# Two attention layers and experts on one core: slots of exp tiles chosen by the planner, and layer 1's softmax sums on TensorE

## The chip, the core and the metric

The kernel runs on one core of one Trainium2 chip. A core has five engines that work side by side and wait for each other by semaphores: TensorE (PE: matmuls, and PEld for loading weights), VectorE (DVE), ScalarE (ACT), GpSimd (POOL) and SyncE (SP, which here only issues DMAs). TensorE writes to PSUM; the other tiles lie in SBUF. The metric is the device time of one execution in microseconds (us).

## The reference

The input x is 8 images of 256 channels and 32 x 32 pixels, all in float32. Layer 0 is attention of 8 heads of 32 channels, with keys and values from x at four pooled sizes (1024 + 256 + 121 + 25 = 1426 places). Layer 1 is attention of one head of 256 channels over the 1024 pixels as tokens, followed by eight experts of three products each, weighted by a gate that is taken from the mean over the images. Cut to what matters:

```python
# layer 0, after a group norm of x; k and v: pooled, convolved, layer-normed
attn = softmax(einsum('bhqd,bhkd->bhqk', q_g, k) * 32 ** -0.5)
out_att = einsum('bhqk,bhkd->bhqd', attn, v)
...                                   # mixed by a small constant attention, then projected
x = x + out
# layer 1
t = tokens(x)
t = t + softmax(q1 @ k1.T * 256 ** -0.5) @ v1        # q1, k1, v1 from layernorm(t)
h = relu(bn(layernorm(t) @ W1[e])); h = relu(bn(h @ W2[e])); y = h @ Wo[e]
t = t + sum over e of gate[f, e] * y
```

## The kernel before

Almost every instruction is recorded through one object, Flow, so the profile gives nearly all of them the same line (L671, inside Flow's call); a reader goes by tile names and not by lines. Flow keeps a clock for each engine (`now`), and for each tile a time at which it will be ready and one at which it will have been read. Flow.cost prices an instruction; Flow.transfer prices a DMA. Every engine executes its instructions in the order in which they are recorded.

Layer 0's scores are the backbone. The loop at the end of `attention` runs over image b, head group c (four heads), half of the queries (512) and key chunk kc (up to 128 places). A step records `scores`: four products into the single PSUM tile sc, and one exp of 128 x 2048 into a tile pt. One step later it records `values`: four products into pv with the exps as operand. There are 352 such exps, and 8 of the last 18 keys (ptail). The softmax sum over the keys needs the exp tiles added up: the odd chunk's tile is added onto the even chunk's by a GpSimd DMA with accumulation (`add`), VectorE adds the pairs (`sums`), and a product with ones sums over the partitions. `normalise` turns that total into rec (transpose, reciprocal of 16 columns, transpose) and multiplies att by it. pt has six slots. An exp tile's slot comes free when its last reader is done: the adding DMA for an odd tile, a VectorE add for an even one, the ones-product for the first.

Between the steps, Flow.step lets other threads record work as filler: convolutions and keys for the next image (VectorE's taps on acc), queries, the projection, and all of layer 1 as far as its input is there. A thread yields what it needs next, an engine and tiles, and is resumed when Flow's clock says that these are near; TensorE's filler is limited by a credit for each step. Flow.finish records whatever is needed until a condition holds.

Which slot a new tile gets is decided in two places. Flow.tile assumes, for its own account, the slot that comes free first. The tile pool, which only knows that a tag has six slots, places the tile itself, and nothing ties the two together.

Layer 1 runs as two threads. `layer1` normalises tokens, makes v and y, and records for each of 32 blocks of 256 queries four exp tiles p1 of two key chunks each (tag p1, six slots). `outputs` sums them: four VectorE adds into s, one product with ones, a reciprocal of 128 x 256 from PSUM; then the products with v, the multiplication by the reciprocal, the residual, a store, and the norm. In both layers ScalarE sums up the totals and their reciprocals by Copy with accum_out into the tables hi and lo; at the end of the kernel these are compared with a limit, and a general path runs if a value is too large.

When the last scores are done, the experts begin, interleaved with what is left of layer 1. Until the gates are known, expert layers are computed ahead, each as four products of 512 columns, and kept in DRAM (h2d); afterwards most are seven products of 256 columns (Strassen's scheme) with sums on VectorE. The expert part works on the banks named bank and y.

Of the kernel before, what the change touches and what calls it, by code (L numbers as in the profile page):

```python
# [36 lines left out]
NEAR = {"DVE": 1.5, "ACT": 2.0, "POOL": 1.0, "SP": 10.0}  # L37
BUFS = {"sm": 2, "sx": 1}
# [15 lines left out]
class Kit:  # L54
# [6 lines left out]
    def tile(self, pool, shape, tag, bufs=None):  # L61
        self.n += 1
        return pool.tile(shape, F32, tag=tag, name=f"{tag}_{self.n}", bufs=bufs)
# [594 lines left out]
class Flow:  # L658
# [27 lines left out]
    def __init__(self, tc, kit):  # L686
# [10 lines left out]
        self.threads = []  # L697
        self.cut = {}
# [6 lines left out]
    def tile(self, pool, shape, tag, bufs=1):  # L705
        t = self.kit.tile(pool, shape, tag, bufs=bufs)
        slots = self.slots.setdefault(tag, [None] * bufs)
        i = min(range(bufs), key=lambda i: self.end(slots[i]))
        self.ready[t.name] = self.end(slots[i])
        slots[i] = t.name  # L710
        if tag in BUFS:
            self.open.add(t.name)
        return t

# [51 lines left out]
    def note(self, engine, op, ins, args, kwargs):  # L766
# [35 lines left out]
        if "dma" in op:  # L802
            both = out.space == DRAM and srcs[0].space == DRAM
            size = 4e-3 * out.shape[0] * out.free_size() if out.space != DRAM else 4e-3 * srcs[0].shape[0] * srcs[0].free_size()
            lag = self.transfer(engine, end, size * (0.0054 if engine == "POOL" or both else 0.003))
# [8 lines left out]
    def transfer(self, queue, at, work):  # L814
# [10 lines left out]
        return 1.7 + left[mine] + min(left[mine], left[other]) + self.served - at  # L825
# [88 lines left out]
def attention(tc, kit, f, outer, ended, nb, consts, x, t1, t2, hn, bounds, vecs, q_t, kv_t, proj_t, gqk_t, wqk, wqkv, vecs1, w1_d, w1c, gate_d, wrc, vecs2, bnvec, w2_d, h2d, between, pre, held):  # L914
# [6 lines left out]
    with ExitStack() as ctx:  # L921
# [41 lines left out]
        ident, grp = kit.ident, con[:, K_GRP : K_GRP + P]  # L963
        heads = T(l1, [P, P + DH], "res", bufs=2)
# [28 lines left out]
        def mix():  # L993
# [48 lines left out]
            yield ve(wa)  # L1042
            rs = T(wp, [P, 2], "wars")
# [24 lines left out]
            yield ve(ps)  # L1068
            raw = T(l1, [P, 2, C], "s")
# [111 lines left out]
        pmaps = [T(pool_, [P, NK], f"p{i}") for i, pool_ in enumerate((between, work))]  # L1181
# [70 lines left out]
        def first_keys(half):  # L1252
# [3 lines left out]
            for m in range(2):  # L1256
# [15 lines left out]
                f.act.activation(acc[:, half * 512 : half * 512 + 512], ps, AF.Identity, bias=db(m, 0))  # L1272
            large.append(("keys", half))
# [326 lines left out]
        def sums(n, pairs):  # L1600

            for i in range(1, NKC // 2):
                yield until(lambda: len(pairs) > i)
                for j in range(0, 4, 2):
                    s = pairs[0][:, j : j + 2, :]
                    yield ve(s, pairs[i])
                    f.ve.tensor_tensor(s, s, pairs[i][:, j : j + 2, :], ALU.add)
            yield until(lambda: normalised[0] == n)
            yield pe(pairs[0], tag="sm")
            total = small()  # L1610
            for j in range(4):
                f.pe.matmul(
                    total[DH * j : DH * j + DH, :], lhsT=kit.ones[:, :DH], rhs=pairs[0][:, j, :], start=True, stop=True
                )
            return total

        def normalise(b, c, sl, total, n):
# [5 lines left out]
            f.act.activation(total, total, AF.Copy, accum_out=hi[:, column[n] : column[n] + 1])  # L1623
            one = T(work, [P, 16, 1], "one")
            f.ve.reciprocal(one, turned[:, :, 0:1])
            f.ve.transpose(turned, one.to_broadcast([P, 16, DH]))
            f.ve.tensor_tensor(att, att, rec, ALU.mult)
            yield act(rec)
            f.act.activation(rec, rec, AF.Copy, accum_out=lo[:, column[n] : column[n] + 1])

        def project(b):
            if b == nb - 1:
                last = T(work, [P, 2, HW], "pt", bufs=6)
                f.sp.dma_start(last, x[b].rearrange("(k p) n -> p k n", p=P))
# [19 lines left out]
            if b == nb - 1:  # L1654
                f.sp.dma_start(t1[b], last)
            projected[0] += 1
# [92 lines left out]
        def outputs():  # L1749

            for i in range(4 * nb):
# [5 lines left out]
                s = T(l1, [P, 2, C], "s")  # L1757
                yield ve(*p1[:2])
                f.ve.tensor_tensor(s, p1[0], p1[1], ALU.add)
                for g in range(2, 4):  # L1760
                    yield ve(p1[g])
                    f.ve.tensor_tensor(s, s, p1[g], ALU.add)
                f.ve.tensor_tensor(s[:, 0, :], s[:, 0, :], s[:, 1, :], ALU.add)
                yield pe(s, tag="sm")
                ps = small()
                f.pe.matmul(ps[:, :C], lhsT=kit.ones, rhs=s[:, 0, :], start=True, stop=True)
                yield ve(ps)
                rec = T(l1, [P, C], "rec1")
                n = 8 * (i // 4) + 4 + i % 4
                f.act.activation(ps[:, C:], ps[:, :C], AF.Copy, accum_out=hi[:, n : n + 1])  # L1770
                f.ve.reciprocal(rec, ps[:, :C])
# [980 lines left out]
```

## Time and profile before

| | us |
|---|---|
| median of 3 runs (3258.67 to 3266.59) | 3259.01 |
| the profiled execution | 3261.05 |
| its span, first to last instruction | 3259.2 |
| TensorE busy with matmuls | 3056.5 |
| VectorE busy | 2406.7 |
| ScalarE busy | 1682.6 |
| GpSimd busy | 1240.7 |

Layer 0's scores run from 78 to about 1900 us of the span, the experts' banks from 2013 on. In the trace every float32 product appears as two records (two passes), so counts of matmuls there are twice those of the program. A product with 32 weight columns is marked 128*32; four of them run side by side in the array's column groups. In lists of waits, a line names who waited, for whom, the total, how often, and the longest. In tables by stretches, each engine's busy time is followed by its number of records; PEclk is the mean granted share of TensorE's clock.

### The profile page before, as it was taken

How to read it: one execution, taken by the hardware profiler on the slowest of the kernel's cores; microseconds unless marked ns; L12 is line 12 of the kernel's file. 1: busy time of each engine (PE TensorE's matmuls, PEld its weight loads, DVE VectorE, ACT ScalarE, POOL GpSimd, SP SyncE). 2: the span in 40 equal slices, each digit the busy share in tenths (PEclk: the TensorE clock that was granted, in tenths of full speed). 3: DMA queues.
4: the chain of work that ended last, by engine and by line, in shares of the span. 5: the costliest groups of instructions: out<-in, count | busy, mean ns of one | idle time of the engine just before them, and what ended most of it. 6: DMA issues, size and time to landing. Idle time of an engine off the chain costs nothing.

```text
span 3259.2 us, 55911 instructions
## 1 busy us (share of the span) xinstructions
PE 3056.5 (94%) x22330; PEld 1789.3 (55%) x22330; DVE 2406.7 (74%) x4117; ACT 1682.6 (52%) x2301; POOL 1240.7 (38%) x1327
## 2 busy tenths in 40 slices
PE   8778799999979989989999999999999999999998
PEld 4322234334325334424333356777888888888887
DVE  5886786987877888969754544447888887777776
ACT  4566566666645657657665533333333334444443
POOL 3211413224222232232121112007655667777776
PEclk9899999999989999989999999999999999999999
DMA  1376657665664565565676645225444430000000
GB/s 54 86 153 156 125 124 155 137 148 111 141 145 84 128 151 113 137 143 111 141 182 126 144 111 207 94 88 171 146 149 149 149 117 20 20 20 33 20 14 21
DMA packets 115710, 368.68 MB, mean 113 GB/s; under 512 B 14305, under 2 KB 40233, under 8 KB 92209
## 3 DMA queue, kind: packets, MB, share of 16 engines
q0 software_dynamic: 28608, 179.85, 28.5%
q1 hardware_dynamic: 83472, 183.19, 16.7%
q8 instruction: 178, 2.92, 0.4%
q10 hardware_dynamic: 3360, 1.97, 0.2%
q14 instruction: 92, 0.75, 0.1%
HBM read 116.12 MB, written 83.40 MB: 61 GB/s over the span
## 4 chain that ended last, share of the span: by engine, by line
PE 49%; DVE 6%; DMA 3%; issue 2%; ACT 2%; POOL 1%; SPq 0%; DVEq 0%; POOLq 0%; ACTq 0%
PE bank L671 20%; PE y L671 10%; PE sm L671 9%; PE sx L671 4%; PE sc L671 3%; PE pv L671 3%; DVE h L671 2%; DMA pt<-pt 2%; ACT pt L671 1%; DVE acc L671 1%; DVE u L671 1%; DVE c L671 1%; DVE pt L671 1%; DVE t L671 0%; DMA t<-res 0%
## 5 line engine op out<-in xcount | busy, mean ns | idle before, releaser
L671 ACT ACTIVATE pt<-sc 128x2048 f32<-128x2048 f32 x352 | 660.9, 1877 | 296.7 <-PE sc L671 204.3
L671 DVE SCALAR_TENSOR_TENSOR acc<-p,vec,acc 128x961 f32<-128x961 f32 (+3 forms) x960 | 562.2, 594 | 35.1 <-ACT acc L671 9.4
L671 PE MATMUL sc<-q,kn 32*128 32x512 f32 (+1 forms) x3072 | 428.5, 662 | 125.1 <-ACT pt L671 121.8
L671 DVE TENSOR_TENSOR pt<-pt,pt 128x1024 f32<-128x1024 f32 x320 | 391.9, 1271 | 148.3 <-DMA pt<-pt 123.7
L671 PE MATMUL pv<-pt,vt 128*32 128x512 f32 x2816 | 390.9, 628 | 1.7 <-ACT vt L671 1.2
L671 ACT ACTIVATE h<-h,bnvec 128x512 f32<-128x512 f32 x450 | 340.4, 805 | 61.8 <-DVE h L671 53.1
L671 ACT ACTIVATE p1c<-bank 128x256 f32<-128x256 f32 x225 | 86.2, 383 | 553.5 <-PE bank L671 553.2
L671 POOL TENSOR_TENSOR rstd<-rstd,mhalf 128x4 f32<-128x4 f32 (+2 forms) x88 | 106.6, 1211 | 651.6 <-DVE rstd L671 560.2
L671 POOL DMA_DIRECT2D pt<-pt x160 | 146.3, 916 | 465.4 <-ACT pt L671 376.7
L671 DVE TENSOR_TENSOR h<-p1c,bank 128x512 f32<-128x512 f32 x225 | 153.3, 682 | 200.2 <-PE bank L671 196.5
L671 PEld LDWEIGHTS sc<-q,kn 32*128 32x128 f32 (+1 forms) x3072 | 115.7, 182 | 324.4 <-ACT pt L671 223.2
L671 POOL TENSOR_TENSOR tm<-h,tm 128x256 f32<-128x256 f32 x208 | 239.2, 1150 | 16.3
L671 DVE TENSOR_TENSOR h<-u,bank 128x256 f32<-128x256 f32 x450 | 229.2, 550 | 7.7
L671 PEld LDWEIGHTS pv<-pt,vt 128*32 128x32 f32 x2816 | 56.3, 109 | 281.3 <-issue 262.1
L671 POOL TENSOR_TENSOR tm<-h 128x512 f32<-128x512 f32 x104 | 133.2, 1281 | 202.6 <-ACT h L671 198.5
L671 DVE TENSOR_TENSOR h<-h,gate 128x1024 f32<-128x1024 f32 x128 | 199.9, 1561 | 0.5 <-ACT h L671 0.5
L671 PE MATMUL y<-t,s3e 128*128 128x256 f32 x768 | 187.0, 379 | 3.1 <-POOL t L671 1.7
L671 PE MATMUL bank<-t,s1e 128*128 128x256 f32 x726 | 178.1, 381 | 2.6 <-DVE t L671 2.4
L671 POOL TENSOR_TENSOR t<-h,t 128x256 f32<-128x256 f32 x214 | 169.5, 792 | 16.8
L671 POOL TENSOR_TENSOR t<-h 128x512 f32<-128x512 f32 x107 | 136.1, 1272 | 98.1 <-DVE h L671 77.4
L671 DVE TENSOR_TENSOR u<-h,bank 128x512 f32<-128x512 f32 x225 | 154.7, 688 | 24.7 <-PE bank L671 1.4
L671 PEld LDWEIGHTS y<-t,s3e 128*128 128x128 f32 x768 | 145.7, 190 | 24.0 <-POOL t L671 2.5
(376 smaller groups left out, 5557.5 us busy)
## 6 DMA issues: line engine op xcount, KB each, us to landing
pt<-pt POOLq DMA_DIRECT2D x160, 1024.0 KB, 7.7
h<-h SPq DMA_DIRECT2D x123, 512.0 KB
xi<-in_x_dram SPq DMA_DIRECT2D x16, 512.0 KB
t<-t SPq DMA_DIRECT2D x8, 1024.0 KB
res<-t SPq DMA_DIRECT2D x32, 256.0 KB
t<-res SPq DMA_DIRECT2D x32, 256.0 KB
hn<-res SPq DMA_DIRECT2D x32, 256.0 KB
hn<-hn SPq DMA_DIRECT2D x16, 512.0 KB
```

Source lines behind the costliest of these rows:

```text
L671: ins = fn(*args, **kwargs)
```

## The change

Tiles of the tags in OWN (pt and p1) get their slot from Flow: each slot is a tag of its own with one buffer, and Flow.tile takes the slot that by its account comes free first among those that are not held. A tile is held from its recording until `drop` is called on it after its last use has been recorded. Before an exp of layer 0 is recorded, Flow.finish records other work until a place of pt is vacant. The price of a DMA in the account changes: 0.0036 us per KB for one issued by GpSimd (before 0.0054), and 2.2 us of fixed time (before 1.7).

In layer 1 the four adds, the product with ones and the large reciprocal are replaced. Eight products with 32 columns of ones sum the eight chunks over their tokens, those of tile g into column group g; VectorE transposes the result in blocks of 32; four products of 8 columns with a stacked 32 x 32 identity (i32, a new constant tile) join the four groups; VectorE copies and inverts 8 columns and spreads them by a transpose. In both layers the accumulating copies now read a small tile two that holds total and reciprocal, both into one column, and are recorded later and under a yield of their own. The projection's start moves from `unit` into `normalise`. The tiles p0 and p1 of the convolution are renamed map0 and map1. The diff, without further drops and renamings:

```diff
@@ -35,6 +35,7 @@
 MARGIN = 1.5
 AHEAD = {"DVE": 4.0, "ACT": 2.0, "POOL": 1.0, "SP": 10.0}
 NEAR = {"DVE": 1.5, "ACT": 2.0, "POOL": 1.0, "SP": 10.0}
+OWN = {"pt", "p1"}
 BUFS = {"sm": 2, "sx": 1}
 AHEAD3 = 3
 PACE2 = 8.0
@@ -58,8 +59,10 @@
         self.nc = nc
         self.n = 0
 
-    def tile(self, pool, shape, tag, bufs=None):
+    def tile(self, pool, shape, tag, bufs=None, slot=None):
         self.n += 1
+        if slot is not None:
+            return pool.tile(shape, F32, tag=f"{tag}.{slot}", name=f"{tag}_{self.n}", bufs=1)
         return pool.tile(shape, F32, tag=tag, name=f"{tag}_{self.n}", bufs=bufs)
 
     def rstd(self, out, var, eps):
...
@@ -703,14 +707,24 @@
         self.credit, self.port = [0.0, 0.0], 0.0
 
     def tile(self, pool, shape, tag, bufs=1):
-        t = self.kit.tile(pool, shape, tag, bufs=bufs)
         slots = self.slots.setdefault(tag, [None] * bufs)
-        i = min(range(bufs), key=lambda i: self.end(slots[i]))
+        own = tag in OWN
+        i = min((i for i in range(bufs) if slots[i] not in self.held), key=lambda i: self.end(slots[i]))
+        t = self.kit.tile(pool, shape, tag, bufs=bufs, slot=i if own else None)
+        if own:
+            self.held.add(t.name)
         self.ready[t.name] = self.end(slots[i])
         slots[i] = t.name
         if tag in BUFS:
             self.open.add(t.name)
         return t
+
+    def drop(self, *tiles):
+
+        self.held.difference_update(map(self.key, tiles))
+
+    def vacant(self, tag):
+        return any(name not in self.held for name in self.slots.get(tag, [None]))
 
     def end(self, name):
 
@@ -802,7 +816,7 @@
         if "dma" in op:
             both = out.space == DRAM and srcs[0].space == DRAM
             size = 4e-3 * out.shape[0] * out.free_size() if out.space != DRAM else 4e-3 * srcs[0].shape[0] * srcs[0].free_size()
-            lag = self.transfer(engine, end, size * (0.0054 if engine == "POOL" or both else 0.003))
+            lag = self.transfer(engine, end, size * (0.0036 if engine == "POOL" else 0.0054 if both else 0.003))
         for n in {*outs, self.key(out)}:
             self.ready[n] = max(self.ready.get(n, 0.0), end + lag)
             self.writer[n] = "DMA" if "dma" in op else engine
@@ -822,7 +836,7 @@
         for i in range(2):
             left[i] = max(0.0, left[i] - done - max(0.0, span - both))
         left[mine] += work
-        return 1.7 + left[mine] + min(left[mine], left[other]) + self.served - at
+        return 2.2 + left[mine] + min(left[mine], left[other]) + self.served - at
 
     @staticmethod
     def key(a):
@@ -961,6 +975,8 @@
         nc.scalar.dma_start(pjw, proj_t.rearrange("(k p) f -> p k f", p=P))
         con = kit.con
         ident, grp = kit.ident, con[:, K_GRP : K_GRP + P]
+        i32 = T(l1, [P, DH], "i32")
+        nc.scalar.dma_start(i32, consts[:, K_I32:K_SEL])
         heads = T(l1, [P, P + DH], "res", bufs=2)
         nc.scalar.dma_start(heads, consts[:, K_HEAD:K_SEL])
         head = heads[:, :P]
...
@@ -1612,6 +1633,7 @@
                 f.pe.matmul(
                     total[DH * j : DH * j + DH, :], lhsT=kit.ones[:, :DH], rhs=pairs[0][:, j, :], start=True, stop=True
                 )
+            f.drop(pairs[0])
             return total
 
         def normalise(b, c, sl, total, n):
@@ -1620,16 +1642,20 @@
             turned = rec.rearrange("p (j i) -> p j i", i=DH)
             yield ve(total)
             f.ve.transpose(rec, total)
-            f.act.activation(total, total, AF.Copy, accum_out=hi[:, column[n] : column[n] + 1])
-            one = T(work, [P, 16, 1], "one")
-            f.ve.reciprocal(one, turned[:, :, 0:1])
-            f.ve.transpose(turned, one.to_broadcast([P, 16, DH]))
+            two = T(work, [P, 32, 1], "two", bufs=2)
+            f.ve.tensor_copy(two[:, :16], turned[:, :, 0:1])
+            f.ve.reciprocal(two[:, 16:], turned[:, :, 0:1])
+            f.ve.transpose(turned, two[:, 16:].to_broadcast([P, 16, DH]))
             f.ve.tensor_tensor(att, att, rec, ALU.mult)
-            yield act(rec)
-            f.act.activation(rec, rec, AF.Copy, accum_out=lo[:, column[n] : column[n] + 1])
+            normalised[0] += 1
+            if c and sl.start:
+                f.spawn(project(b), 1)
+            yield act(two)
+            f.act.activation(T(work, [P, 32, 1], "bin"), two, AF.Copy, accum_out=hi[:, column[n] : column[n] + 1])
 
         def project(b):
             if b == nb - 1:
+                yield until(lambda: f.vacant("pt"))
                 last = T(work, [P, 2, HW], "pt", bufs=6)
                 f.sp.dma_start(last, x[b].rearrange("(k p) n -> p k n", p=P))
             for m in range(2):
...
@@ -1754,22 +1781,30 @@
                 yield until(lambda: scaled[0] >= i - 1)
                 res = T(l1, [P, 2, C], "res", bufs=2)
                 f.sp.dma_start(res, t1[b][:, :, q])
-                s = T(l1, [P, 2, C], "s")
-                yield ve(*p1[:2])
-                f.ve.tensor_tensor(s, p1[0], p1[1], ALU.add)
-                for g in range(2, 4):
-                    yield ve(p1[g])
-                    f.ve.tensor_tensor(s, s, p1[g], ALU.add)
-                f.ve.tensor_tensor(s[:, 0, :], s[:, 0, :], s[:, 1, :], ALU.add)
-                yield pe(s, tag="sm")
+                yield pe(*p1, tag="sm")
                 ps = small()
-                f.pe.matmul(ps[:, :C], lhsT=kit.ones, rhs=s[:, 0, :], start=True, stop=True)
+                for u in range(2):
+                    for g in range(4):
+                        f.pe.matmul(
+                            ps[DH * g : DH * g + DH, :C],
+                            lhsT=kit.ones[:, :DH],
+                            rhs=p1[g][:, u, :],
+                            start=u == 0,
+                            stop=u == 1,
+                        )
+                yield ve(ps)
+                parts = T(l1, [P, 8, DH], "s")
+                f.ve.transpose(parts.rearrange("p j i -> p (j i)"), ps[:, :C])
+                yield pe(parts, tag="sm")
+                ps = small()
+                for g in range(4):
+                    f.pe.matmul(ps[DH * g : DH * g + DH, :8], lhsT=i32, rhs=parts[:, :, 0], start=True, stop=True)
                 yield ve(ps)
                 rec = T(l1, [P, C], "rec1")
-                n = 8 * (i // 4) + 4 + i % 4
-                f.act.activation(ps[:, C:], ps[:, :C], AF.Copy, accum_out=hi[:, n : n + 1])
-                f.ve.reciprocal(rec, ps[:, :C])
-                f.act.activation(ps[:, C:], rec, AF.Copy, accum_out=lo[:, n : n + 1])
+                two = T(l1, [P, 16, 1], "two1")
+                f.ve.tensor_copy(two[:, :8], ps[:, :8].unsqueeze(2))
+                f.ve.reciprocal(two[:, 8:], ps[:, :8].unsqueeze(2))
+                f.ve.transpose(rec.rearrange("p (j i) -> p j i", i=DH), two[:, 8:].to_broadcast([P, 8, DH]))
                 yield pe(*p1, v, tag="sm")
                 ps = small()
                 for m in range(2):
@@ -1784,6 +1819,7 @@
                             stop=kc == 7,
                         )
                 taken[0] += 1
+                f.drop(*p1)
                 yield ve(ps, rec)
                 m2 = ps.rearrange("p (m q) -> p m q", m=2)
                 f.ve.tensor_tensor(m2, m2, rec[:, None, :].to_broadcast([P, 2, C]), ALU.mult)
@@ -1791,6 +1827,9 @@
                     f.ve.scalar_tensor_tensor(res[:, m, :], m2[:, m, :], gb[:, m : m + 1], res[:, m, :], ALU.add, ALU.add)
                 f.sp.dma_start(t2[b][:, :, q], res)
                 f.spawn(norm(b, q, res), 5)
+                n = 8 * (i // 4) + 4 + i % 4
+                yield act(two)
+                f.act.activation(T(l1, [P, 16, 1], "bin1"), two, AF.Copy, accum_out=lo[:, n : n + 1])
 
         scaled = [0]
 
...
@@ -1963,9 +2003,6 @@
         def unit(b, c, sl, n, pairs):
             total = yield from sums(n, pairs)
             yield from normalise(b, c, sl, total, n)
-            normalised[0] += 1
-            if c and sl.start:
-                f.spawn(project(b), 1)
 
         atts = {}
         f.spawn(chain(*map(keys_and_values, range(nb))), 2)
@@ -2008,6 +2045,7 @@
                     f.finish(lambda: key_parts[0] > 3 * b + 2 and (b, 1) in qs and (b or len(asked) == 4))
                     tail_scores(b)
                 else:
+                    f.finish(lambda: f.vacant("pt"))
                     pts[i] = scores(b, c, sl, kc)
                 f.step()
             if i and steps[i - 1][3] < NKC - 1:
@@ -2021,6 +2059,7 @@
                 f.finish(lambda: kc1 // 4 in vts[b1])
                 values(b1, c1, kc1, pts[i - 1], pv)
                 if kc1 % 2:
+                    f.drop(pts[i - 1])
                     add(kc1, pts.pop(i - 1), pts[i - 2])
                     pairs.append(pts.pop(i - 2))
                 if kc1 == NKC - 2:
```

## The prediction

> **What bounds the kernel now.** I read, in this order: the page's busy shares and slices, a table of busy time by stretches of the run, the waits in total, the waits of ScalarE's exps, and the chain of waits around single stalls.
>
> ```profile
> PE 3056.5 (94%) x22330; PEld 1789.3 (55%) x22330; DVE 2406.7 (74%) x4117; ACT 1682.6 (52%) x2301; POOL 1240.7 (38%) x1327
> ...
> PEclk9899999999989999989999999999999999999999
> ```
>
> The shares say TensorE first, VectorE second. The table by stretches (start:end, length, then busy time of PE, PEld, DVE, ACT and POOL, granted clock, DMA share) says where TensorE is not busy:
>
> ```profile
> 78.00:1900.00 1822.00, 1659.34 (x16223) 645.17 (x16226) 1391.32 (x2602) 1152.01 (x1402) 473.46 (x538) 0.97 0.62 134
> 1900.00:2015.00 115.00, 112.72 (x456) 77.64 (x449) 45.43 (x83) 31.06 (x59) 20.46 (x41) 1.00 0.44 142
> ...
> 2230.00:3259.00 1029.00, 1009.44 (x4657) 882.92 (x4656) 813.88 (x1146) 387.09 (x636) 694.10 (x671) 1.00 0.22 74
> ```
>
> Of 202.7 us without a matmul, 162.7 lie in the stretch 78 to 1900, which is layer 0's attention with layer 1 as its filler. From 1900 on TensorE is 98% busy: only its own work counts there. In the first stretch the clock is below one too. What ends TensorE's waits, and ScalarE's:
>
> ```profile
> PE sc L671 <- ACT pt L671: 121.8, 99, 6.2
> ...
> ACT sm L671 <- DVE rec L671: 82.0, 42, 4.0
> ...
> ACT pt L671 <- DMA pt<-pt: 71.7, 22, 7.3
> ...
> ACT sx L671 <- DVE rec L671: 38.3, 17, 5.7
> ```
>
> The score tile sc is single: the next scores wait for the exp that empties it (1.88 us). So anything that holds an exp back stops TensorE once its filler is used up. Two things hold exps. The first is a slot of the tile pt, still being read by the GpSimd DMA that adds an odd exp tile to its even partner. The chain shows two such stalls in a row:
>
> ```profile
> 1401.33 7.46 DMA pt<-pt
> ...
> 1408.90 1.89 ACT pt L671
> ...
> 1411.18 8.05 DMA pt<-pt
> ...
> 1419.31 1.89 ACT pt L671
> ```
>
> Following every TensorE gap over 0.8 us back to its releaser, and that one's releaser, gives for this stretch: 46.2 us behind exps that waited for a pt slot; about 17 us behind exps queued on ScalarE behind the normaliser's copies, which themselves waited for VectorE (11.4 us for the transpose or reciprocal into rec, 5.8 us for the multiplication of att); 28.2 us in 28 gaps of about 1 us, where a step had no filler and the scores simply waited out one exp.
>
> **What the skill says.** The Trainium skill, "TensorE: Matmul & The Clock Gate", Part 1: the array falls to half clock after an idle window of about 3.4 us and comes back after about as long busy. The trace agrees: its clock records show half clock in pieces of 3.41, 6.83, 10.24 and 20.48 us, and the stretch after the stalls above reads 0.51:
>
> ```profile
> 1412.00:1433.00 21.00, 17.12 (x75) 3.22 (x76) 7.32 (x7) 10.06 (x9) 9.68 (x15) 0.51 0.61 132
> ```
>
> So a stall costs its idle time and then half of the busy time in such a piece. "PSUM — Partial Sum Buffer", Engine vs sequencer instructions, calls the ScalarE, VectorE and GpSimd queues strict FIFO: an accumulating copy that waits for VectorE holds the exp behind it, as read above (the 82.0 and 38.3 us). "DMA: Bandwidth & Descriptors", Anatomy of one DMA, prices a GpSimd-issued DMA at 2.0 us plus bytes at 436 GB/s, 4.4 us for 1 MB; the page measures 7.7 us for these adding DMAs, and I use 7.7. "TensorEngine Tiling (Array Packing)", Instruction Overhead: a product of one column costs as much as one of 60; used below for a tiny product.
>
> **The change, part by part.**
>
> *Places of pt and p1.* I compared the two instruction streams. For each exp that reuses a slot last read by an adding DMA, I counted how many exps lie between. Before: 5 slots reused one exp after the DMA's issue, 29 after two, 124 after three or four. After: none, 1, and 157. In the trace of before, 17 of the 21 exps that I could tie to such a DMA had a distance of one or two; four had three (DMAs that took 9 to 12 us). At a mean step of 5.06 us (1822/360) three steps are 15 us, against 7.7. Of the 46.2 us of TensorE idle, 33.8 belong to distances of one or two, 9.5 to three, 2.9 to a VectorE add. After: 9.5 x 157/124 = 12, and 2.9, so 15 are left and 31 go. What is late next is the filler: the steps without any fall from 59 to 45, which takes 28.2 x 14/59 = 7 us. All half-clock pieces of 78 to 1900 sum to 116 us. Those that follow slot stalls are 68.3 us, of which TensorE was busy in 52.6; half of it, 26, is lost. In the ratio 31/46.2, 18 us come back. Parts: 31 + 7 + 18 = 56; from 33 (idle alone, half of it) to 80.
>
> *The shorter price of adding DMAs in the planner.* 1,049 KB now count 2.2 + 3.8 = 6.0 us, before 1.7 + 5.7 = 7.4; measured 7.7. VectorE's adds therefore stand nearer to their DMA: with at most one exp between, 97 of 160 before and 135 after. Mean waits of such adds in the trace of before, by exps between: 1.08 us for none, 1.02 for one, 0.79 for two, 0.44 for three. With the counts after (59, 76, 19, 6) that is 159 us of VectorE waits instead of 141. The 18 us are hidden by what VectorE gains below; behind each waiting add stand the taps on acc, the reciprocals and the transposes, and TensorE's fillers wait for those. Without cover they would cost 18. I take 0; the upper bound is the second rival.
>
> *Layer 1's sums, 32 times.* VectorE loses 0.709 (first add) + 2 x 0.706 + 0.43 + 1.755 (reciprocal of 128x256) = 4.3 us, 138 in all. It gains two transposes of 128x256 (half of the 128x512 row's 711 ns and a little, 0.4 each), a copy of 8 columns (0.152 for the row of 2 columns) and a reciprocal of 8 (0.25 for the row of 16): 1.2 us, 38; layer 0's small copy adds 5. Net about -95 us of 1391. VectorE is not the bound, so I count nothing for it beyond the cover just used. TensorE gains. A wave of four column-group products of 256 columns takes 0.43 us (32 pass records, 16 products, in 1.73):
>
> ```profile
> 1284.71 1.73 PE sm L671 x32
> ```
>
> Two waves replace one: 32 x 0.43 = 13.8 us. Four tiny products of 8 columns are 8 passes. The nearest row is one of the tile y:
>
> ```profile
> L671 PE MATMUL sm<-bqkv,y x8: 250/250/271, 128.9 to 129.7; 128*128 128x1 f32 x8
> ```
>
> It has a pass of one column every 0.11 us, with 128 weight columns where these have 32. The skill's 60 cycles at 2.4 GHz are 0.025, an estimate from its page. I take 0.06: 32 x 8 x 0.06 = 15 us, from 6 to 28. Two more hand-overs between TensorE and VectorE per sum replace one (gaps of 1.9 us behind an s add in the trace): I take 4 us, from -2 to 10.
>
> *Bounds and normaliser.* The four accumulating copies over 256 and 512 columns with their 0.19 us reads (layer 1: 0.375 + 0.388 + 0.37 per sum, layer 0: 0.58 + 0.63 + 0.37 per unit; 87 us of ScalarE) become two small ones, an estimated 0.4 us with read, 26 us. More important, they are now handed to ScalarE when their input is ready and after the multiplication, so they don't hold exps: the 17 us go, and half of 5.8 us after the stall at 389. 20 us; from 10, if other copies take their place. In layer 0 the next unit's sum no longer waits for the second copy.
>
> *The rest.* By the counts of both programs, six expert layers more are computed directly (four products of 512 columns, 3.45 us, against seven of 256, 3.02: 6 x 0.43 = 2.6 us), and 18 more h tiles go through DRAM on SP's queue, beside matmuls. The i32 load on ScalarE's queue lies in the start. Slots by name and drops issue nothing. The demand that a pt place be vacant before an exp moves VectorE's adds ahead of it; reuses whose last reader is a VectorE add only one exp away fall from 17 to 10, so I count no loss.
>
> Sum: -31 - 7 - 18 - 20 + 13.8 + 15 + 4 + 2.6 = -40.6. The profiled execution took 3261.05 us (span 3259.2), so 3220; the median shown, 3259.01, is 2 us lower: 3218.
>
> **Rivals.** *Late DMAs keep the slots (3252).* Distances are counted in the program; in the trace GpSimd often issues late, stuck before a power for rstd (560 us waited for VectorE in all). If a third of the slot and clock gain comes true (16 of 49) and the normaliser's 20 shrinks to 12, the gain is 16 + 7 + 12 against 35 of added work: nearly nothing, and with a few new gaps 3252. For it: issue gaps of 6 and 9 us before such powers in the chain. Against: two thirds of the waits had distances of one or two.
>
> *VectorE becomes the bound (3293): the slower side.* If an add with no exp between waits for the whole landing, 7.7 less half a step of 2.5, that is 59 x 5.2 = 307, and with about one microsecond for the others some 400 us instead of 141. VectorE has 1391 - 91 = 1300 us busy in this stretch (about 29 of the 32 sums lie in it) and 224 us of other waits (431 idle, less 141, less the 66 us behind ScalarE's copies that go). In a stretch of 1780 it decides from 256 us of DMA waits on; at 400 it is 144 over, of which I let half be swallowed by the other waits: 3218 + 75 = 3293. For it: 135 near adds. Against: in before near adds waited about 1 us only, since VectorE arrives late at them.
>
> *More than counted (3185).* All slot stalls go with their clock, 46 + 26 = 72 instead of 49, and the tiny products cost 6 instead of 15: 32 us more.
>
> **How the numbers follow.** Main case 0.50 at 3218, own range 3192 to 3246 from the bounds above; late DMAs 0.16; VectorE 0.22; more gain 0.12. Within 0.3% (about what a measurement of this kernel can tell from no change) is 3249 to 3269. Faster: 0.50 + 0.12 + a third of 0.16 = 0.67. Same: half of 0.16 and a little, 0.10. Slower: 0.22 and the rest, 0.23. The range 3182 to 3285 leaves out a bit of the fourth case and more than half of the third.
>
> **What would show it.** Right: exps' waits on DMA pt<-pt fall from 71.7 us to about 20; ScalarE's waits on rec vanish; TensorE's waits on exps fall from 121.8 to about 70; PEclk has fewer 8s; PE busy rises by some 30 us less the clock's return. Wrong: VectorE's waits on DMA pt<-pt above 250 us, tiny products over 0.9 us per sum, or TensorE gaps behind acc, kn or kt instead of pt.

## The result, and the profile after

| | before | after |
|---|---|---|
| median of 12 runs each | 3258.84 us (3256.43 to 3266.59) | 3263.57 us (3256.36 to 3273.8) |
| ratio, 95% interval | | 1.0006 (0.9997 to 1.0016) |
| profiled execution | 3261.05 us, span 3259.2 | 3256.36 us, span 3253.9 |
| VectorE's waits for adding DMAs (pt<-pt and pt<-ptail) | 141.3 us | 243.4 us |
| exps' waits for a pt slot (DMA pt<-pt) | 71.7 us | 12.7 us |

The change makes no difference that a measurement can tell. The profiled execution of after is the fastest of its twelve, so its view lies 7 us below the median. The page of the changed kernel (busy us, share of the span and instructions of each engine; the clock in tenths by slice):

```profile
PE 3071.9 (94%) x23382; PEld 1781.1 (55%) x23382; DVE 2307.1 (71%) x4111; ACT 1629.8 (50%) x2167; POOL 1195.2 (37%) x1291
...
PEclk9899899999999999999999999999999999999999
...
L674 ACT ACTIVATE pt<-sc 128x2048 f32<-128x2048 f32 x352 | 660.8, 1877 | 307.2 <-PE sc L674 252.3
...
L674 DVE TENSOR_TENSOR pt<-pt,pt 128x1024 f32<-128x1024 f32 x320 | 389.7, 1264 | 255.7 <-DMA pt<-pt 233.2
...
pt<-pt POOLq DMA_DIRECT2D x160, 1024.0 KB, 7.8
```

The row of VectorE's adds read, before:

```profile
L671 DVE TENSOR_TENSOR pt<-pt,pt 128x1024 f32<-128x1024 f32 x320 | 391.9, 1271 | 148.3 <-DMA pt<-pt 123.7
```

VectorE has 100 us less to do (2406.7 before) and ScalarE 53 less (1682.6), yet VectorE now stands idle for 255.7 us in front of its adds into pt, where it was 148.3. The adding DMA itself is as slow as before, 7.8 us against 7.7. The waits in total of after (us, times, longest), beside those shown of before:

```profile
DVE pt L674 <- DMA pt<-pt: 233.2, 73, 9.8
...
PE sc L674 <- ACT pt L674: 88.2, 74, 6.6
...
ACT bin L674 <- DVE two L674: 50.5, 27, 4.3
...
ACT kt L674 <- DVE tshift L674: 23.2, 11, 7.4
...
ACT map L674 <- DVE acc L674: 22.3, 7, 6.0
...
ACT pt L674 <- DMA pt<-pt: 12.7, 4, 7.7
...
ACT vt L674 <- DVE tshift L674: 11.0, 6, 3.4
```

The waits that the change was to remove are gone: exps for a slot from 71.7 to 12.7, the copies on rec entirely. In their place VectorE waits 109.5 us longer for pt<-pt (123.7 before), and ScalarE waits for VectorE's small results: tshift for kt and vt 34.2 us (3.6 + 1.2 before). Where that reaches TensorE is seen in one stretch of the timeline of after (start, duration, engine, instruction, then idle time before it and releaser):

```profile
985.89 2.36 DVE L674 TENSOR_TENSOR pt<-pt,pt 128x1024 f32<-128x1024 f32 x2 [6.09 <-DMA pt<-pt]
...
988.17 1.39 DVE L674 BATCH_NORM_STATS2 tst<-kt 128x6 f32<-128x256 f32 x4
...
990.51 1.93 POOL L674 TENSOR_TENSOR rstd<-rstd,mhalf 128x4 f32<-128x4 f32 x1 [10.84 <-DVE rstd L674]
...
992.41 0.90 POOL L674 DMA_DIRECT2D pt<-pt  x1
...
992.47 0.16 DVE L674 SCALAR_TENSOR_TENSOR tshift<-tmean,rstd 128x4 f32<-128x4 f32 x1 [0.93 <-POOL rstd L674]
...
992.73 1.09 ACT L674 ACTIVATE kt<-kt,tshift,rstd 128x256 f32<-128x256 f32 x2 [1.87 <-DVE tshift L674]
...
995.19 1.85 ACT L674 ACTIVATE pt<-sc 128x2048 f32<-128x2048 f32 x1
...
997.09 1.14 PE L674 MATMUL sc<-q,kn 32*128 32x512 f32 x8 [1.36 <-ACT pt L674]
```

VectorE stands 6.09 us in front of one add. Behind it wait the statistics of kt, GpSimd's power, the next adding DMA in GpSimd's queue, and the scaling of kt, which stands on ScalarE in front of the next exp: that exp starts at 995.19 though its scores were done about 1.6 us earlier, and TensorE idles 1.36 us. The Trainium skill, "PSUM — Partial Sum Buffer", Engine vs sequencer instructions, has the queues of ScalarE, VectorE and GpSimd as strict FIFO (first in, first out). The trace agrees: the 6.09 us in front of one add pass through all three to TensorE.

The stretches of after (columns as before):

```profile
78.00:1900.00 1822.00, 1677.49 (x17175) 648.55 (x17175) 1332.26 (x2620) 1109.33 (x1295) 473.46 (x538) 0.97 0.63 136
...
2230.00:3259.00 1029.00, 1002.23 (x4593) 870.34 (x4591) 808.69 (x1138) 376.73 (x620) 664.55 (x656) 1.00 0.28 96
```

TensorE is 18 us busier in the first stretch than before (1659.34), partly because the layer-0 attention ends earlier: the last score product falls at 1859.9 us, before at 1897.4. Whole span: TensorE's idle time fell by 20.7 us (202.7 to 182.0) and its busy time rose by 15.4, together the 5.3 us by which the spans differ. Half of the busy time that lies in the half-clock pieces of the clock records is an estimate of what they cost: 50.3 us before and 41.8 after. So some 8.5 us of clock came back and, with the 15.4, some 24 us of work were added.

### The profile page after: what moved, and what is told of

Same layout as the page of the kernel before. It is cut to its first block, busy times and chain, and to the rows that moved or that the text cites. A ratio compares the mean times of both kernels' runs of the same rounds, so it can differ in the third digit from the quotient of the medians.

```text
span 3253.9 us, 57863 instructions
## 1 busy us (share of the span) xinstructions
PE 3071.9 (94%) x23382; PEld 1781.1 (55%) x23382; DVE 2307.1 (71%) x4111; ACT 1629.8 (50%) x2167; POOL 1195.2 (37%) x1291
## 4 chain that ended last, share of the span: by engine, by line
PE 50%; DVE 5%; issue 2%; DMA 2%; ACT 1%; POOL 1%; DVEq 0%; ACTq 0%; POOLq 0%
PE bank L674 21%; PE sm L674 11%; PE y L674 10%; PE sc L674 3%; PE pv L674 3%; PE sx L674 2%; DMA pt<-pt 2%; DVE h L674 1%; ACT pt L674 1%; DVE u L674 1%; DVE c L674 1%; DVE acc L674 1%; DVE pt L674 1%; POOL t L674 0%; DVE t L674 0%
## 5 line engine op out<-in xcount | busy, mean ns | idle before, releaser
L674 DVE SCALAR_TENSOR_TENSOR acc<-map,vec,acc 128x961 f32<-128x961 f32 (+3 forms) x960 | 563.0, 595 | 33.8 <-ACT acc L674 8.0
L674 DVE TENSOR_TENSOR pt<-pt,pt 128x1024 f32<-128x1024 f32 x320 | 389.7, 1264 | 255.7 <-DMA pt<-pt 233.2
L674 ACT ACTIVATE h<-h,bnvec 128x512 f32<-128x512 f32 x438 | 331.3, 805 | 64.3 <-DVE h L674 56.7
L674 DVE TENSOR_TENSOR h<-u,bank 128x256 f32<-128x256 f32 (+1 forms) x438 | 222.9, 550 | 7.5
L674 POOL TENSOR_TENSOR tm<-h,tm 128x256 f32<-128x256 f32 x196 | 222.5, 1135 | 15.4
L674 POOL TENSOR_TENSOR tm<-h 128x512 f32<-128x512 f32 x98 | 126.0, 1286 | 191.2 <-ACT h L674 191.2
L674 PE MATMUL sm<-p,v 128*32 128x256 f32 (+1 forms) x2184 | 178.3, 380 | 2.4 <-DVE two L674 2.4
L674 PE MATMUL sm<-y,t 128*32 128x256 f32 (+1 forms) x2104 | 177.3, 379 | 1.1 <-DVE res L674 1.1
L674 POOL TENSOR_TENSOR t<-h 128x512 f32<-128x512 f32 x101 | 128.3, 1270 | 124.2 <-DVE h L674 91.2
```

Source lines behind the costliest of these rows:

```text
L674: ins = fn(*args, **kwargs)
```

## The experiments

About 45 us are missing. The recorded expectations name their theories by letters, and a letter can mean something else in a later group; the text uses those of the group it is in. In the first group, A: the places gain, and TensorE's extra products for layer 1 eat half of it. B: the waits only move from ScalarE to VectorE and cost as much there; with the old price they should shrink. C: the reordered normaliser and its small copies cost it. All ratios are against the kernel before, run beside each. "Near adds" is the count, in the program, of VectorE adds with no exp between them and the DMA whose sum they read (36 in the kernel before).

### Parts alone: four kernels

`slots_only` has places and price, with the sums and normaliser of before:

```diff
-                yield pe(*p1, tag="sm")
+                s = T(l1, [P, 2, C], "s")
+                yield ve(*p1[:2])
+                f.ve.tensor_tensor(s, p1[0], p1[1], ALU.add)
...
-            f.ve.tensor_copy(two[:, :16], turned[:, :, 0:1])
-            f.ve.reciprocal(two[:, 16:], turned[:, :, 0:1])
+            f.act.activation(total, total, AF.Copy, accum_out=hi[:, column[n] : column[n] + 1])
+            one = T(work, [P, 16, 1], "one")
+            f.ve.reciprocal(one, turned[:, :, 0:1])
```

> Only the places by the account, the drops and the new DMA price; layer 1's sums and the accumulating copies as before. Theory A (the places gain some 35 us of TensorE idle time and clock, and layer 1's extra products, 16.4 + 3.7 us of TensorE, eat the half of it): about 3240 us, TensorE busy about 3040, exps' waits on DMA pt<-pt below 20 us, VectorE's waits on DMA pt<-pt above 200. Theory B (the waits only move from ScalarE to VectorE, and VectorE, now late, holds TensorE back as much): 3255 to 3265. Theory C (what costs is the reordered normaliser and its small copies, not the products): 3225 to 3235.

`no_slots` has the new sums and normaliser, with the pool's own places and the old price (a wait for the projection is also stated three lines earlier; that line alone moves no instruction in the changed kernel, nor in new_price_no_slots below):

```diff
-OWN = {"pt", "p1"}
+OWN = set()
...
-            lag = self.transfer(engine, end, size * (0.0036 if engine == "POOL" else 0.0054 if both else 0.003))
+            lag = self.transfer(engine, end, size * (0.0054 if engine == "POOL" or both else 0.003))
...
-        return 2.2 + left[mine] + min(left[mine], left[other]) + self.served - at
+        return 1.7 + left[mine] + min(left[mine], left[other]) + self.served - at
...
+                    f.finish(lambda: projected[0] >= b1)
```

> The new layer 1 sums and the reordered copies, with the tile pool's own places and the old DMA price; the wait for the projection is recorded before the last pair is handed over. Theory A: before plus 20 us of products less 5 to 10 us that the copies gain: 3268 to 3275, exps' waits on DMA pt<-pt 40 to 70 us. Theory B: about 3263, like the changed kernel. Theory C: 3280 or more.

`old_price` is the changed kernel with the two price lines of before, as in the diff above, and nothing else:

> The changed kernel with the old DMA price (1.7 us and 0.0054 per KB) in the account. Of the adds 36 have no exp between them and their DMA's issue, against 59. Theory A leaves the price small: 3255 to 3265. Theory B (VectorE's waits, 233 us, are what ate the gain): VectorE's waits on DMA pt<-pt fall to about 150 us, the exps' stay below 20, and the time falls to 3235 to 3250.

`dve_sums` is the changed kernel with layer 1's sums, reciprocal and accumulating copies of before:

```diff
-                for u in range(2):
-                    for g in range(4):
-                        f.pe.matmul(
...
+                    f.ve.tensor_tensor(s, s, p1[g], ALU.add)
+                f.ve.tensor_tensor(s[:, 0, :], s[:, 0, :], s[:, 1, :], ALU.add)
+                yield pe(s, tag="sm")
...
+                f.ve.reciprocal(rec, ps[:, :C])
```

> The changed kernel with layer 1's sums back on VectorE (four adds, one product, the large reciprocal, two accumulating copies); places, price and normaliser as changed. Theory A: 20 us below the changed kernel, about 3243, TensorE busy 20 us less. Theory B: VectorE gets some 90 us of work back beside its 233 us of waits, so 3270 or more. Theory C: like the changed kernel, about 3263.

Measured (medians and ratios with intervals; the last columns from each profile and program):

| kernel | us | ratio | VectorE waits for pt<-pt | near adds |
|---|---|---|---|---|
| slots_only | 3268.23 | 1.0021 (1.0011 to 1.0031) | 208.5 | 66 |
| no_slots | 3252.85 | 0.9976 (0.9968 to 0.9985) | 138.7 | 37 |
| old_price | 3216.17 | 0.9857 (0.9841 to 0.9874) | 163.6 | 36 |
| dve_sums | 3288.21 | 1.0093 (1.0068 to 1.0118) | 209.4 | 60 |
| (changed kernel) | 3263.57 | 1.0006 (0.9997 to 1.0016) | 233.2 | 59 |

Two numbers in the planner's price are worth 47 us: with the old ones the changed kernel takes 3216. A falls in all four kernels; going back to the old sums makes it 25 us slower, where A had 20 us faster. C falls in the three for which it gave a figure. B is right for dve_sums (3270 or more) and in direction for old_price, but the price does more than B said (3235 to 3250); slots_only came out 3 us above B's range and no_slots 10 below its figure, so the waits do not cost just what the places gain. The waits of old_price:

```profile
DVE pt L674 <- DMA pt<-pt: 163.6, 50, 14.4
...
PE sc L674 <- ACT pt L674: 76.8, 73, 4.4
...
ACT pt L674 <- DMA pt<-pt: 18.1, 6, 7.4
...
ACT map L674 <- DVE acc L674: 13.4, 4, 5.4
...
ACT kt L674 <- DVE tshift L674: 4.2, 3, 1.6
```

VectorE waits 70 us less than in after, kt waits 4.2 instead of 23.2, vt has left the list, and TensorE's waits on exps fall by 11.4. Grouping TensorE's gaps over 0.8 us between 78 and 1950 us by what released them, and by what held that one, gives:

| gaps of TensorE behind | before | after | old_price |
|---|---|---|---|
| exps that waited for a slot (DMA) | 43.3 | 10.3 | 10.0 |
| exps queued behind other work of ScalarE | 29.9 | 38.3 | 26.1 |
| exps' bare round trip of about 1 us, no filler left | 28.2 | 24.4 | 23.4 |
| other (most are fillers that themselves wait) | 41.5 | 50.5 | 32.9 |

So the slots gain the same at both prices, and the bare round trips are alike. What the new price gives back is in the second and the last row (12.2 and 17.6 us). Followed one step further back, 22.4 us of the second row in after come from ScalarE waiting for VectorE (for tshift, two or acc), and 9.6 us in old_price: that is the whole difference of the row. Of the last row's 50.5, one gap of 7.4 us at 117 us is a product that follows VectorE's copy into diag. The two spans differ by 37.2 us; besides these rows 4.6 us of it is busy time, of which 2.5 by half clock.

### The price without the places, the places without the rest, and other prices

`new_price_no_slots` keeps the new price and everything else, with `OWN = set()`:

> The changed kernel with the pool's own places, but the new DMA price: 63 adds with no exp between them and their DMA's issue, and 5 reuses of a slot at distance one or two instead of 24 with the old price. Theory B (the price alone makes VectorE wait, and costs some 45 us with or without the places): 3275 to 3300, VectorE's waits on DMA pt<-pt above 200 us. Theory E (the price is bad only together with the held slots, because adds are then forced ahead of an exp): about 3253, as without places and with the old price.

`slots_old` is slots_only with the two price lines of before (the places are then the only part of the change):

> The places by the account alone: old DMA price, layer 1's sums, copies and normaliser as before. Theory B (places gain 37 us whatever the sums): 3222 to 3232, exps' waits on DMA pt<-pt below 20 us, VectorE's waits on DMA pt<-pt about 150. Theory F (the places gain only when VectorE is relieved of layer 1's sums and so can keep up): 3245 to 3262.

`price_up` prices adding DMAs above what is measured, 5.7 + 3.5 = 9.2 us for 1,049 KB, and has the early wait for the projection of no_slots:

```diff
-        return 2.2 + left[mine] + min(left[mine], left[other]) + self.served - at
+        return 3.5 + left[mine] + min(left[mine], left[other]) + self.served - at
```

> The changed kernel with the old rate of 0.0054 and a fixed time of 3.5 us, so that a 1,049 KB adding DMA is priced 9.2 us: only 17 adds have no exp between, 78 have two or more. Theory B with dose: VectorE's waits on DMA pt<-pt below 100 us, and 3205 to 3220. Theory G (there is a best price near the measured 7.8 us; beyond it slots come free later and the demand for a vacant place takes over): 3220 to 3245. Theory H (any other order differs by some tens of us, by chance): anything from 3215 to 3265, with no relation to VectorE's waits.

`near_a` asks how much a mere shuffle of the order is worth: old price, with 1.8 in place of 1.7:

> The changed kernel with the old rate and a fixed time of 1.8 us instead of 1.7: nearly the same price, another order in detail. Theory B: within 8 us of the kernel with the old price, 3208 to 3224. Theory H (chance of the order): more than 12 us away from 3216.

| kernel | us | ratio | VectorE waits for pt<-pt | near adds |
|---|---|---|---|---|
| new_price_no_slots | 3279.12 | 1.0052 (1.0035 to 1.0068) | 253.7 | 63 |
| slots_old | 3240.77 | 0.9938 (0.9917 to 0.9958) | 135.3 | 47 |
| price_up | 3226.11 | 0.9894 (0.9874 to 0.9915) | 114.9 | 17 |
| near_a | 3225.88 | 0.9892 (0.9871 to 0.9912) | 181.2 | 31 |

In this group B (the price costs with or without places) is right for new_price_no_slots, and E (only together with held slots) falls. slots_old lies between its two ranges: the places gain, but less with the old sums. price_up fell into G's range and not B's. near_a came out 9.7 us from old_price, between B's 8 and H's 12. It sets the scale: a tenth of a microsecond in the price moves the time by 10 us, through another order of the same work. Single differences of that size say little. But the price has the same sign in all three pairs: 3216 to 3264 with the whole change (+47), 3241 to 3268 with the places alone (slots_old to slots_only, +27), 3253 to 3279 without places (no_slots to new_price_no_slots, +26). So it needs neither the places nor the new sums to do harm. The waits of new_price_no_slots:

```profile
DVE pt L674 <- DMA pt<-pt: 253.7, 77, 10.7
...
PE sc L674 <- ACT pt L674: 90.7, 77, 6.7
...
ACT pt L674 <- DMA pt<-pt: 30.1, 10, 5.1
ACT kt L674 <- DVE tshift L674: 29.7, 10, 8.9
```

price_up answers whether dearer is better still. VectorE's waits fall to the lowest of all, the time does not:

```profile
ACT pt L674 <- DMA pt<-pt: 24.0, 8, 6.2
ACT pt L674 <- DVE pt L674: 23.1, 9, 4.3
```

With the adds set late, exps wait for a VectorE add that still reads their slot (23.1 us, in after 3.8); 15.3 us of TensorE's gaps lie behind such exps. The old price, 7.4 us for a measured 7.8, stands between the two; a price of just 7.8 was not run.

### Which half of the price, and which part of the rest

Two answers to why the new price hurts were open. B: the sum counts as ready too early, so that VectorE's add is set too near to its DMA. I: other times in the account do it, such as the partner's slot, which counts as free too early. Both kernels keep the new price and put 1.4 us (for 1,049 KB) back on one of the two only:

```diff
-        lag = 0.15
+        lag, late = 0.15, 0.0
...
+            if engine == "POOL" and not both:
+                late = 0.0018 * size - 0.5
...
-            self.ready[n] = max(self.ready.get(n, 0.0), end + lag)
+            self.ready[n] = max(self.ready.get(n, 0.0), end + lag + late)
```

This is `late_ready`; `late_read` adds `late` to the line of `self.read[n]` instead.

> The changed kernel with the new DMA price, but the sum that an adding GpSimd DMA writes counts as ready by about the old price (1.4 us later for 1,049 KB); the slot that it reads still counts as free by the new one. Of the adds 41 have no exp between, as with the old price (36). Theory B (VectorE's adds stand too near their DMAs): VectorE's waits on DMA pt<-pt about 170 us, and 3210 to 3230. Theory I (the new price costs by the slots' or other times in the account): 3250 to 3270.

> The mirror: the slot that an adding DMA reads counts as free by about the old price, the sum that it writes as ready by the new one; 58 adds have no exp between. Theory B: like the changed kernel, 3250 to 3270, VectorE's waits on DMA pt<-pt above 210 us. Theory I: 3210 to 3230.

`sums_norm0_old` has places, old price and the new sums, with layer 0's normaliser of before:

```diff
-            f.ve.tensor_copy(two[:, :16], turned[:, :, 0:1])
-            f.ve.reciprocal(two[:, 16:], turned[:, :, 0:1])
+            f.act.activation(total, total, AF.Copy, accum_out=hi[:, column[n] : column[n] + 1])
+            one = T(work, [P, 16, 1], "one")
+            f.ve.reciprocal(one, turned[:, :, 0:1])
```

> Places by the account with the old price, layer 1's new sums, and layer 0's normaliser with its two accumulating copies as before. Between the kernel with the old sums and copies (3241) and the one with all new (3216). If the normaliser's copies are worth the 20 us of my prediction: about 3236, and the sums, of which I counted 35 us of cost, nearly nothing. If the sums' relief of VectorE is what counts: about 3220.

`mix_old_price` has places, old price and the new normaliser; in layer 1 the four adds stay on VectorE, one ones-product leaves the total on all partitions, and only the inversion is made on the transposed form:

```diff
+                f.ve.tensor_tensor(s[:, 0, :], s[:, 0, :], s[:, 1, :], ALU.add)
+                yield pe(s, tag="sm")
...
+                f.pe.matmul(ps[:, :C], lhsT=kit.ones, rhs=s[:, 0, :], start=True, stop=True)
...
+                parts = T(l1, [P, 8, DH], "parts")
+                f.ve.transpose(parts.rearrange("p j i -> p (j i)"), ps[:, :C])
...
+                f.ve.reciprocal(two[:, 8:], parts[:, :, 0:1])
```

> Places, old price, normaliser as changed; layer 1's four adds stay on VectorE with one product, but the 256-column reciprocal becomes transpose, 8 columns inverted, transpose. TensorE has 20 us less to do than in the kernel with the old price, VectorE some 80 us more. Theory A (TensorE's own work counts): 3196 to 3205, the best version. Theory B (VectorE's time counts in the attention stretch, busy or waiting): 3220 to 3240.

| kernel | us | ratio | VectorE waits for pt<-pt | near adds |
|---|---|---|---|---|
| late_ready | 3230.25 | 0.9890 (0.9866 to 0.9913) | 170.0 | 41 |
| late_read | 3276.16 | 1.0046 (1.0029 to 1.0063) | 237.8 | 58 |
| sums_norm0_old | 3222.86 | 0.9886 (0.9869 to 0.9902) | 208.6 | 39 |
| mix_old_price | 3202.68 | 0.9814 (0.9798 to 0.9831) | 150.0 | 36 |

The first two separate B from I. Waits of late_ready:

```profile
DVE pt L674 <- DMA pt<-pt: 170.0, 64, 11.1
...
PE sc L674 <- ACT pt L674: 75.6, 75, 3.4
```

and of late_read:

```profile
DVE pt L674 <- DMA pt<-pt: 237.8, 71, 12.9
...
PE sc L674 <- ACT pt L674: 79.1, 66, 5.4
...
ACT bin L674 <- DVE two L674: 67.3, 32, 6.1
...
ACT map L674 <- DVE acc L674: 37.7, 12, 5.3
```

The old landing time for the sum takes 63 us of VectorE's waits and 33 of the 47 us away, as B said (about 170 us, 3210 to 3230). The old time for the slot leaves the waits where they were and the kernel 13 us slower than the changed one, 6 above B's range and far from I's. So the price acts, in the main, through the place of VectorE's adds. late_ready also keeps the new 2.2 us for every other DMA, so these can have no more than a part in the remaining 14 us, which stay open. By the classes of gaps above, late_ready has 17.3 us behind queued exps and 46.4 of other gaps, late_read 34.4 and 69.7. The pair late_ready and late_read also shows that TensorE's own line for exps (75.6 and 79.1) hardly tells the two apart: idle time up to the last score product does, 133.5 against 162.6 us, and it holds gaps behind late fillers too.

sums_norm0_old holds a warning: it waits 208.6 us for DMAs and takes 3223. The total of VectorE's waits is a sign of the trouble and not its measure; what counts is what stands behind the waiting add.

mix_old_price is the fastest, 0.9814 (0.9798 to 0.9831), faster than both kernels. Its page:

```profile
PE 3050.1 (95%) x22408; PEld 1786.1 (56%) x22408; DVE 2392.1 (75%) x4244; ACT 1634.9 (51%) x2172; POOL 1224.6 (38%) x1321
```

And that of old_price:

```profile
PE 3067.3 (95%) x23334; PEld 1781.7 (55%) x23334; DVE 2299.4 (71%) x4110; ACT 1631.4 (51%) x2166; POOL 1189.0 (37%) x1285
```

Against old_price it gives VectorE 93 us more and TensorE 17 us less, and is 13.5 us faster, a little more than a shuffle of the order may give. Of its two theories, A (TensorE's own work counts) is right and B (VectorE's time counts, busy or waiting) falls. Its span is 11.9 us shorter: 17.2 us less busy time, 5.3 us more idle. That fits with where the work lies: after the last score TensorE has only some 21 to 30 us of idle left in each of these kernels, so a product taken off it is mostly taken off the time.

## Why the prediction was wrong, step by step

**The price of adding DMAs is the step that failed.** It read: "Without cover they would cost 18. I take 0; the upper bound is the second rival." Measured: 47 us with the whole change, 26 and 27 in the two other pairs. Two errors are in it. The waits were worked out from class means of the kernel before (1.08 us for an add with no exp between), which gave 159 us; after shows 243.4. The counts were right: 59 adds with no exp between and 76 with one. The means were not, and the second class more than the first: adds with no exp between wait 1.32 us in after, those with one exp 1.85, where before had 1.08 and 1.02. That second class makes 63 of the 84 us that are missing. Before, 21 of its 61 adds waited at all, in after 42 of 76; with the old price (old_price) its mean is 0.99. So a mean depends on where the price sets the adds and does not carry over to another price. And "hidden by what VectorE gains" treated its time as one sum. An in-order engine that waits 6 us holds the tshift or acc behind it at that moment, however idle it is elsewhere: VectorE has 71% busy in after and still delays exps. The second rival had the mechanism, but set it to decide from 256 us of waits on, where VectorE would be full; it does harm earlier, at about two thirds of the rival's 75 us, and the prediction's own sign for it, waits for pt<-pt above 250 us, did not show in after (233.2).

**Places of pt and p1: mechanism right, size too large.** The step gave 31 us of stalls, 7 of fillers and 18 of clock. Exps' slot waits fell to 12.7 us (about 20 forecast), and TensorE's gaps behind them by 33.0 (43.3 to 10.3; 31 forecast). In time, at the old price, the places are worth 19 us with the old sums (3259.7 beside it to 3240.8, ratio 0.9938, 0.9917 to 0.9958) and 37 with the new (no_slots to old_price). Fillers: bare round trips went from 28.2 us to 24.4 in after and 23.4 in old_price, 4 to 5 us of the 7. Clock: about 8.5 us back against 18 forecast. The first rival, late DMAs that keep the slots, falls with the 12.7 us; its own sum gives 3259 (35 us of gain against 35 of work), not 3252.

**Layer 1's sums: TensorE's side nearly right in sum, VectorE's side wrong.** The occupancy of the sum products (start to next start) rose by 16.4 us, 13.8 forecast. The tiny products took 3.7 us in all, 15 forecast: 256 passes at 14.5 ns, not 60. The direct expert parts cost 4.6, 2.6 forecast. These 24.7 us account for the roughly 24 us of added work. VectorE's busy time fell by 99.6 us in all (95 forecast). That was counted at nothing, yet the exchange gained more than the products cost: at the old price, new sums take 3240.8 to 3222.9, 18 us off, where the step had 33 us on (13.8 + 15 + 4). With the new price the same exchange is 25 us (dve_sums to the changed kernel). But mix_old_price shows that neither the 2 x 32 product waves nor the adds taken off VectorE were what helped; it keeps the adds there and is faster. That points to the 1.755 us reciprocal and the accumulating copies as the part that pays; a kernel with only these two edited was not run, so it is argued and not shown.

**Normaliser: 20 us forecast, sign not settled.** At the old price the new one of layer 0 takes 6.7 us off (sums_norm0_old to old_price); with the new price and old sums it adds 20 (slots_only to dve_sums). The first is less than near_a's shuffle. The waits on rec are gone as forecast; those of bin on two (50.5 us) took their place, less than half of the 120.3 that there were.

**What the two errors make together.** The prediction's 3218 is what old_price gives, 3216. That is in part luck: places and normaliser were taken too large, the sums with the wrong sign. Only the price, counted as nothing, is missing as one term of the size of the whole error, 46 us.

Two things remain open. Whether the rate or the fixed part of the price does the harm was not tried. And the scatter of some 10 us between orders that differ by almost nothing has no cause shown here; it limits how finely the parts can be told apart.

## What to carry to other kernels

A planner that sets an in-order engine's instruction by the expected landing of a DMA needs one near the landing that the profile shows. For a measured 7.8 us, the 7.4 of before was the best of those tried; 6.0 cost 26 to 47 us, in the whole change as much as all the rest gained; 9.2 cost about 10, the size of a mere shuffle. When an edit moves a waiting instruction earlier, do not take its wait from what such waits were in the old order. Here neither the old means (1.02 us, where 1.85 came) nor the whole landing less half a step (the rival's 5.2 us, where 1.32 came) held. Price a wait by what stands behind it. Undo constants of a planner first: they are the cheapest experiment and may hold the largest effect.

## What was not expected of the hardware

Four products with 32 weight columns and 8 moving columns, eight passes, took 0.08 us from their start to the next group's in the lines below, and all 256 passes 3.7 us. The Trainium skill, "TensorEngine Tiling (Array Packing)", Instruction Overhead, has about 60 cycles for any small product, 25 ns by the estimate used before. The whole trace shows 14.5 ns of TensorE's time for each pass when four go side by side, 58 ns for four; that four share the time is no contradiction to a figure for one. The prediction's 60 ns a pass was an estimate between the page's figure and the 0.11 us of a product of one column with 128 weight columns. The timeline of TensorE in after:

```profile
601.75 0.25 PE L674 MATMUL sm<-s,i 128*32 128x8 f32 x8
601.83 3.64 PE L674 MATMUL sx<-p,v 128*32 128x256 f32 x64
```

And the same changed kernel took from 3256.36 to 3273.8 us over twelve runs, with a mean granted clock of 0.984 in the fastest and 0.979 in the slowest: a difference of 0.5% that would be 16 of the 17 us, and more than some of the parts told apart above. It does not go strictly with the time (a run of 3265.16 us had 0.984 too), and what changes the clock from run to run is not shown.
